# Attention block on one Trainium2 core: residual loads four chains ahead in six buffers, and a later place for the bias on POOL

## The chip, the cores and the metric

The kernel runs on one core of one Trainium2 chip. The metric is the device time of one execution in microseconds; the time before is the median of three runs. The engines are called PE (TensorE, matrix products), DVE (VectorE), ACT (ScalarE), POOL (GpSimd) and SP (SyncE, which here only issues DMAs).

## What is computed

An input x of 4 images with 512 channels and 48 x 48 points goes through a group norm, an attention with 8 heads over the 2304 points of its image, a projection, and is added to the result:

```
hn = _group_norm(x, gn_scale, gn_bias)
qkv = jnp.einsum('oc,bchw->bohw', qkv_w, hn) + qkv_b[None, :, None, None]
...
w = jnp.einsum('bhct,bhcs->bhts', q * scale, k * scale)
w = jax.nn.softmax(w, axis=-1)
a = jnp.einsum('bhts,bhcs->bhct', w, v).astype(jnp.float32)
a = a.reshape(b, c, hh, ww)
out = jnp.einsum('oc,bchw->bohw', proj_w, a) + proj_b[None, :, None, None]
return x + out
```

The change touches the last two lines alone: how x (the residual) and `proj_b` (the bias) get to the projection's result.

## The kernel before

The 8 heads of an image are taken as 4 pairs, so there are 16 pairs in all. A pair's 2304 query points are cut into blocks, four of 512 and one of 256 (`QBLOCKS`). A block is worked off in bursts of three score tiles: six bursts for a block of 512, three for the block of 256. In a burst PE makes scores (L1083), ACT their exponentials (L1090), DVE sums these (`add`, L1139 and L1144), and PE multiplies them with the values two bursts later (L1108). The main loop (L1530) walks through all bursts; `n` is the burst's number, and `now[0]` holds it.

All other work is put beside the bursts from a queue, `beside`, by `fill(n)` (L1477): the products for q, k and v of later pairs, the norm of the next image, and the projection of the image before. The programmer's code fixes the order of all five engines: an engine works off its instructions as the code emitted them, and waits in front of one whose operands are not ready.

When a block is finished, its row sums go a long way round. DVE copies them (`slx`, L1183), SP sends them off by DMA (`sums`, L1186), POOL checks their range in four small steps (`check_sums`, L1205 and L1206, tiles `in` and `tests`), DVE inverts them (L1212), SP sends the inverses to DRAM (`row`, L1214) and back, spread over the partitions (`ib`, L1224), and POOL multiplies (the division, `divide`, L1232). Each step has its burst: check and inversion two bursts after the block, the division two more later.

The projection of a block of 512 points is four chains, one for each 128 output channels; a chain for the block of 256 does two of them. `proj_list` counts them: 18 in an image. A chain is eight matrix products (L970) into one accumulator bank, of which there is only one for all work beside the bursts. Before a block's first chain `begin` (L1023) has ACT and POOL convert the attention's result to the type for four of the products (`att32`, the casts, L960 and L962). After a chain DVE evacuates the bank (L994): it scales the sum and adds it to a residual tile `r` that already holds x plus bias. SP then stores the tile (L997).

The residual tile is made ready thus. `residual` (L904) takes one of `RES` = 4 buffers and has SP load 128 channels of x into it (L915), 256 KB. It then notes in `unbiased` that the bias is due one burst later. `add_bias` (L921) has POOL add it (L926). The main loop calls it near the burst's start (L1545), ahead of the burst's sums, check, division and of `fill`; `proj_run` (L987) calls it at once for a tile that it needs and that has not had its bias yet. The first two loads of an image are issued in `begin` of block 0. Each chain then asks for the load two chains on (`ahead(k + 2)`, L1036), which SP issues in the next burst.

Two more things use these buffers: the projection weights at the start (L568), and one block of the second image (`SPARE`, L509). In the last image three of the five blocks (`in_two`) keep their residual in other buffers, and their loads are issued while the third image is projected, so that POOL then adds two biases a chain. In the tables of the order, `r_0_2` is the residual of block 0, channels from 256 on; the image's number is left out, and the number behind it is the buffer's.

The four projections lie at 637 to 769, 1047 to 1181, 1453 to 1543 and 1545 to 1624 us of the trace. The first three belong to images 0 to 2 and run beside the bursts of the next image; the last is that of image 3.

Of the kernel before, what the change touches and what calls it, by code (L numbers as in the profile page):

```python
# [27 lines left out]
NC = C // P  # L28
# [447 lines left out]
def fast_path(  # L476
# [11 lines left out]
):  # L488
    nc = tc.nc

    RES = NC
    const = ctx.enter_context(tc.tile_pool(name="const", bufs=1))
    xpool = ctx.enter_context(tc.tile_pool(name="xpool", bufs=1))
    qkp = ctx.enter_context(tc.tile_pool(name="qkp", bufs=3))
# [13 lines left out]

    SPARE = {(1, 2): lambda c: ("res", RES), (1, 3): lambda c: (f"a32_{c}", 1)}  # L509

# [56 lines left out]
    def load_wproj(c):  # L567
        wproj[c] = work.tile([P, C], F32, tag="res", bufs=RES, name=f"wproj_{c}")  # L568
        nc.sync.dma_start(wproj[c], proj_wT[bass.ts(c, P), :])
# [314 lines left out]
    now = [0]  # L884
# [14 lines left out]
    def rows_of(dram_tensor, b, j, chunks):  # L899
        o, n = QBLOCKS[j]  # L900
        found = dram_tensor[b, chunks[0] * P : (chunks[-1] + 1) * P, o : o + n]
        return found.rearrange("(m p) n -> p m n", p=P)

    def residual(b, j, chunks):  # L904
        n = QBLOCKS[j][1]
        if in_two(b, j):

            tag = f"x{chunks[0]}_{(j - NQ + 2) % 3}"
            xt = xpool.tile([P, QB], F32, tag=tag, name=f"r_{b}_{j}_{chunks[0]}")
        else:  # L910
            xt = work.tile(
                [P, QB], F32, tag="res", bufs=RES, name=f"r_{b}_{j}_{chunks[0]}"
            )
        xt = xt.rearrange("p (m n) -> p m n", n=n)
        nc.sync.dma_start(xt, rows_of(x, b, j, chunks))  # L915
        res[b, j, chunks[0]] = xt
        unbiased.append((now[0] + 1, (b, j, chunks[0]), chunks))

    unbiased = deque()

    def add_bias():  # L921
        _, key, chunks = unbiased.popleft()
        xt = res[key]
        for i, m in enumerate(chunks):
            bias = bproj[:, m : m + 1].to_broadcast((P, xt.shape[2]))
            nc.gpsimd.tensor_tensor(xt[:, i], xt[:, i], bias, ALU.add)  # L926

    def in_two(b, j):

        return b == B - 1 and j >= NQ - 3  # L930
# [49 lines left out]
    def proj_run(b, j, chunks, pairs=range(NC), bank=None):  # L980

        n = QBLOCKS[j][1]
        if bank is None:
            bank = chain_bank(f"pr_{b}_{j}_{chunks[0]}")
        places = [bank[:, i * n : (i + 1) * n] for i in range(len(chunks))]
        xt = res[b, j, chunks[0]]
        while any(k == (b, j, chunks[0]) for _, k, _ in unbiased):  # L987
            add_bias()
        for m, ps in zip(chunks, places):
            proj_chain(b, j, m, ps, pairs)  # L990

        def evacuate():
            ps = bank[:, : len(chunks) * n].rearrange("p (m n) -> p m n", n=n)
            nc.vector.scalar_tensor_tensor(xt, ps, DOWN, xt, ALU.mult, ALU.add)  # L994

        def store(engine=nc.sync):
            engine.dma_start(rows_of(out, b, j, chunks), xt)  # L997

        return evacuate, store

    def proj_piece(b, j, chunks, pairs=range(NC), ahead=None):
        def run():
            evacuate, store = proj_run(b, j, chunks, pairs)
            evacuate()
            if pairs == LAST:
                finished.add((j, chunks[0]))

            if pairs != FIRST:
                loads.append((now[0] + 1, store))
            if ahead is not None:  # L1010
                loads.append((now[0] + 1, ahead))

        return piece(QB / 290.0 * len(pairs) / NC, run, True, True)

    def proj_pieces(b, j):

        def ahead(k):
            if k < len(proj_list) and not in_two(b, proj_list[k][0]):  # L1020
                residual(b, *proj_list[k])

        def begin():  # L1023
            if in_two(b, j):
                att32(b, j, LAST)
            elif (b, j) == (B - 1, 0):
                att32(b, j, range(len(EARLY), NC))
            else:
                att32(b, j)
            if j == 0:  # L1030
                ahead(0)
                ahead(1)

        pairs = LAST if in_two(b, j) else range(NC)
        chains = [
            proj_piece(b, j, chunks, pairs, lambda k=k: ahead(k + 2))  # L1036
            for k, (jj, chunks) in enumerate(proj_list)
            if jj == j
        ]
        return [piece(0.0, begin)], chains  # L1040
# [293 lines left out]
    for b in range(B):  # L1334
# [20 lines left out]
        if b == B - 1:  # L1355
# [6 lines left out]
            ahead = [  # L1362
                (residual, b, j, chunks)
                for j in (NQ - 2, NQ - 3, NQ - 1)
                for jj, chunks in proj_list
                if jj == j
            ]
# [4 lines left out]
            for j in range(NQ):  # L1372
# [5 lines left out]
            ahead = [  # L1378
                (att32, b, NQ - 3, THIRD),
                (att32, b, NQ - 1, THIRD),  # L1380
                *((att32, b, 0, (c,), True) for c in EARLY),
            ]
# [147 lines left out]
    for n in range(end):  # L1530
        now[0] = n
        idle_once("sync", "scalar", "gpsimd")
        summed = block_at(n - BEHIND - 1)
        if not summed:
            load_due(n)
        wanted(stream[n][0])
        inside = n - BEHIND == soon[1]
        scores(stream[n], (lambda: values(stream[n - BEHIND])) if inside else None)
        if summed:

            rows(*summed, add_up(*summed))
            load_due(n)
        if inside:
            expect_end(kinds.DVE)
        while unbiased and unbiased[0][0] <= n:  # L1545
            add_bias()
        if n > 0:
            add(stream[n - 1])
        filled = summed or n - BEHIND - 1 in soon
        if filled:  # L1550

            fill(n)
        if n >= BEHIND and not inside:
            values(stream[n - BEHIND])
        if block_at(n - BEHIND - 2):
            check_sums(*block_at(n - BEHIND - 2))
            invert(*block_at(n - BEHIND - 2))
        if block_at(n - BEHIND - 3):
            spread(*block_at(n - BEHIND - 3))
        if block_at(n - BEHIND - 4):  # L1560

            divide(*block_at(n - BEHIND - 4))
        if not filled:
            fill(n)
        while joins:
            joins.popleft()()
        if n - BEHIND in soon:
            g, j = stream[n - BEHIND][:2]
            sx = rows(g, j, add_up(g, j))
            if n - BEHIND == soon[1]:  # L1570
                divide_here(g, j, sx, avx[g, j], nc.gpsimd)
        if n - BEHIND - 1 == soon[0]:
            check_sums(g, j)
            invert(g, j)
        if n - BEHIND - 2 == soon[0]:
            spread(g, j)
            divide(g, j)
    g, b, j = NG - 1, B - 1, NQ - 1
    n = QBLOCKS[j][1]
# [18 lines left out]
    ahead, todo = todo[: len(beside)], todo[len(beside) :]  # L1598
# [122 lines left out]
```

## Time and profile before

| | before |
|---|---|
| median of three runs | 1630.75 us |
| lowest and highest run | 1629.93 and 1634.76 us |
| the profiled execution | 1632.66 us |
| its span, first to last instruction | 1630.9 us |
| mean granted clock of PE in it | 0.993 |
| ACT, POOL busy | 1269.4 us, 442.3 us |
| loads of residuals (L915) | 72, median 3.3 us from issue to landing |
| bias additions on POOL (L926) | 80, 93.7 us busy |
| evacuations of projection chains on DVE (L994) | 81 |
| DMA | 82.13 MB, mean 50 GB/s |

A row of the profile's list of waits reads: engine and what it does, for whom it waited, total us, how often, the longest. A row of the timeline has the start in us, the length, the engine, line and operation, out<-in, how many were merged into the row, and in brackets how long the engine had been idle and what ended that. A row of the busy times by stretch has from:to, its length, then for each engine the busy us and the number of instructions, the granted clock of PE, the share of time that the DMA engines were busy, and GB/s. "SPq" is the queue of DMAs that SP issues.

### The profile page before, as it was taken

Reading aid. Unit: us, or ns where it says so; the run is one execution under the profiler, and the core shown is the slowest. Engines: PE = TensorE matmul, PEld = TensorE weight load, DVE = VectorE, ACT = ScalarE, POOL = GpSimd, SP = SyncE. Lnnn points to the kernel's source line nnn. Section 1 sums busy time; section 2 is a strip of 40 time slices with the busy share of each in tenths; the row PEclk is TensorE's granted clock in tenths of the full one; section 3 lists DMA queues with packets and bytes.
Section 4 is the critical chain, followed back from the end, with each engine's and each line's share of the span. In section 5 each row is a group of like instructions: output and inputs, shape, how many; then the busy total and the mean of one; then the engine's idle time right before and its main releaser. Section 6 shows DMA issues by size and latency. Waiting matters only on the chain. (4 is left out here: it accounts for less than half of the span.)

```text
span 1630.9 us, 28897 instructions
## 1 busy us (share of the span) xinstructions
PE 1582.4 (97%) x11526; PEld 681.5 (42%) x11526; DVE 1154.9 (71%) x1302; ACT 1269.4 (78%) x1363; POOL 442.3 (27%) x551
## 2 busy tenths in 40 slices
PE   9988999999999999899999999999999999999896
PEld 3623444443333533445333354444533334434443
DVE  6266768876666668887666666888767676777685
ACT  4166777888888888788888888887878888887784
POOL 1021202311121212642112121354212121128553
PEclk9999999999999999999999999999999999999998
DMA  6001012000000024521000001352100000016323
GB/s 220 1 14 59 15 37 53 12 14 18 14 14 11 15 56 118 147 71 28 11 14 18 14 12 40 114 155 78 31 14 11 14 17 15 14 24 195 114 66 126
DMA packets 94900, 82.13 MB, mean 50 GB/s; under 512 B 50852, under 2 KB 60964, under 8 KB 94756
## 3 DMA queue, kind: packets, MB, share of 16 engines
q1 hardware_dynamic: 92724, 78.35, 17.6%
q8 instruction: 92, 1.51, 0.4%
q10 hardware_dynamic: 1904, 1.84, 0.4%
q14 instruction: 52, 0.43, 0.1%
q0 software_dynamic: 128, 0.01, 0.0%
HBM read 60.70 MB, written 19.17 MB: 49 GB/s over the span
## 5 line engine op out<-in xcount | busy, mean ns | idle before, releaser
L1090 ACT ACTIVATE p<-ps 128x1024 f16<-128x1024 f32 x1296 | 1233.4, 1025 | 329.7 <-PE ps L1083 323.7
L1139 DVE TENSOR_TENSOR acc<-acc,p 128x3072 f16<-128x3072 f16 x270 | 490.5, 1817 | 53.4 <-ACT p L1090 50.8
L812 PE MATMUL pqk<-x,wqkv 128*64 128x512 f32 (+1 forms) x2432 | 514.7, 553 | 4.8 <-DVE k L823 4.7
L1108 PE MATMUL av<-p,v 128*64 128x512 f16 (+1 forms) x2880 | 361.3, 364 | 0.0
L1083 PE MATMUL ps<-q,k 64*128 64x512 f16 (+1 forms) x2880 | 356.5, 358 | 0.4 <-DVE v L872 0.2
L864 PE MATMUL pv<-wqkv,x 128*64 128x256 f32 x2304 | 267.6, 379 | 0.4 <-DVE r L994 0.3
L1205 POOL TENSOR_SCALAR in<-sums 128x8 f32<-128x8 f32 (+1 forms) x158 | 103.5, 655 | 597.8 <-DMA sums<-slx 590.5
L812 PEld LDWEIGHTS pqk<-x,wqkv 128*64 128x64 f32 x2432 | 170.0, 138 | 212.8 <-issue 157.6
L1083 PEld LDWEIGHTS <-k 64*128 64x128 f16 x2880 | 106.6, 94 | 287.8 <-issue 238.4
L1232 POOL TENSOR_TENSOR att<-avx,ib 128x512 f16<-128x512 f32 (+1 forms) x78 | 129.1, 1655 | 355.5 <-DMA ib<-row 334.1
L1108 PEld LDWEIGHTS <-v 128*64 128x64 f16 x2880 | 131.4, 109 | 212.8 <-issue 168.3
L864 PEld LDWEIGHTS pv<-wqkv,x 128*64 128x64 f32 x2304 | 166.2, 137 | 81.9 <-DVE r L994 0.8
L1139 DVE TENSOR_TENSOR acc<-p,p 128x3072 f16<-128x3072 f16 x79 | 142.0, 1797 | 0.0
L1144 DVE TENSOR_TENSOR acc<-acc 128x1024 f16<-128x1024 f16 x156 | 118.6, 760 | 3.3
L926 POOL TENSOR_TENSOR r<-r,bproj 128x512 f32<-128x512 f32 (+1 forms) x80 | 93.7, 1183 | 65.7 <-DMA r<-x_dram 24.5
L823 DVE TENSOR_SCALAR q<-pqk,bqkv 128x512 f16<-128x512 f32 (+1 forms) x77 | 53.4, 694 | 79.2 <-PE pqk L812 78.8
L872 DVE TENSOR_TENSOR v<-pv,bv 128x512 f16<-128x512 f32 x72 | 49.6, 689 | 80.8 <-PE pv L864 80.4
L823 DVE TENSOR_SCALAR k<-pqk,bqkv 128x512 f16<-128x512 f32 (+1 forms) x75 | 52.1, 694 | 74.9 <-PE pqk L812 74.7
L970 PE MATMUL pr<-a,whi 128*128 128x512 f32 (+1 forms) x311 | 96.0, 424 | 4.3 <-POOL a L960 4.2
L970 PE MATMUL pr<-att,wlo 128*128 128x512 f16 (+1 forms) x311 | 76.1, 365 | 19.5 <-DVE r L994 19.1
L1183 DVE COPY slx<-sl 128x512 f32<-128x512 f32 (+1 forms) x79 | 50.5, 640 | 61.8 <-PE sl L1167 61.8
L994 DVE SCALAR_TENSOR_TENSOR r<-pr,r 128x512 f32<-128x512 f32 x75 | 51.4, 686 | 55.7 <-POOL r L926 37.7
(124 smaller groups left out, 544.2 us busy)
## 6 DMA issues: line engine op xcount, KB each, us to landing
r<-x_dram SPq DMA_DIRECT2D x72, 256.0 KB, 3.3
out_dram<-r SPq DMA_DIRECT2D x69, 256.0 KB, 2.3
ib<-row SPq DMA_DIRECT2D x126, 128.0 KB, 3.0
x<-x_dram SPq DMA_DIRECT2D x62, 256.0 KB, 3.9
x<-x_dram SPq DMA_DIRECT2D x16, 128.0 KB, 5.0
sums<-slx SPq DMA_DIRECT2D x128, 2.0 KB, 2.0
ib<-row SPq DMA_DIRECT2D x30, 64.0 KB, 3.1
wqkv<-qkv_wT_dram SPq DMA_DIRECT2D x2, 768.0 KB, 6.9
```

Source lines behind the costliest of these rows:

```text
L812: nc.tensor.matmul(pw[0][lo : lo + D, :n], wqkv[:, c, w0 + lo : w0 + lo + D], hn[b, c, j], start=(c == 0), stop=(c == NC - 1),)
L823: nc.vector.tensor_scalar(qk[g][part][:, o : o + n], pw[0][:, :n], bqkv[:, col : col + 1], SCALE, ALU.add, ALU.mult,)
L864: nc.tensor.matmul(pw[0][lo : lo + D, a, :], hn[b, c, i * P // QB][:, at + lo : at + lo + D], wqkv[:, c, 2 * C + half * C // 2 :][:, : C / ...
L926: nc.gpsimd.tensor_tensor(xt[:, i], xt[:, i], bias, ALU.add)
L970: nc.tensor.matmul(ps[:, :n], w[:, bass.ts(m, P)], a, start=(i == 0), stop=(i == len(steps) - 1),)
L1083: nc.tensor.matmul(ps[:, h, a * n : (a + 1) * n], kt[rows, bass.ts(i, P)], qt[rows, o : o + n], start=True, stop=True,)
L1090: nc.scalar.activation(pt[:, r], ps, AF.Exp)
L1108: nc.tensor.matmul(av[0][lo : lo + D, :n], vv[b, pr // 2][:, i, pr % 2 * P + lo : pr % 2 * P + lo + D], pt[:, r, h, a * n : (a + 1) * n], ...
L1139: nc.vector.tensor_tensor(t, before, pt, ALU.add)
L1144: nc.vector.tensor_tensor(t[:, 0], t[:, 0], t[:, r], ALU.add)
L1205: nc.gpsimd.tensor_scalar(t, sm, limit, None, op)
L1232: nc.gpsimd.tensor_tensor(atts[g][:, o : o + n], avx.pop((g, j))[:, :n], ibs.pop((g, j))[:, :n], ALU.mult,)
```

## The change

There are six residual buffers in place of four. `begin` of block 0 issues the first four loads of an image in place of two, and a chain asks for the load four chains on. The bias is due two bursts after its load in place of one, and the main loop adds due biases after `fill` and the joins, so behind the burst's check, division and casts.

```
-    RES = NC
+    RES = NC + 2
+    LEAD = RES - 2
...
-        unbiased.append((now[0] + 1, (b, j, chunks[0]), chunks))
+        unbiased.append((now[0] + 2, (b, j, chunks[0]), chunks))
...
             if j == 0:
-                ahead(0)
-                ahead(1)
+                for k in range(LEAD):
+                    ahead(k)
...
-            proj_piece(b, j, chunks, pairs, lambda k=k: ahead(k + 2))
+            proj_piece(b, j, chunks, pairs, lambda k=k: ahead(k + LEAD))
...
         if inside:
             expect_end(kinds.DVE)
-        while unbiased and unbiased[0][0] <= n:
-            add_bias()
         if n > 0:
             add(stream[n - 1])
...
         while joins:
             joins.popleft()()
+        while unbiased and unbiased[0][0] <= n:
+            add_bias()
         if n - BEHIND in soon:
```

The lines of the changed kernel are one further on from L916. The order on PE, DVE and ACT is the same in both; it differs on POOL and SP.

On POOL, at the start of the last projection, before:

```order
L960 CAST a_3_0_3_16104<-att_15600 128x512
L926 TENSOR_TENSOR r_0_0_16106<-r_0_0_16106,bproj 128x512
L926 TENSOR_TENSOR r_0_1_16108<-r_0_1_16108,bproj 128x512
L1232 TENSOR_TENSOR att_15600<-avx_1_16004,ib_1_16132 128x512
L926 TENSOR_TENSOR r_0_2_16146<-r_0_2_16146,bproj 128x512
L926 TENSOR_TENSOR r_0_3_16180<-r_0_3_16180,bproj 128x512
```

and in the changed kernel:

```order
L961 CAST a_3_0_3_16104<-att_15604 128x512
L927 TENSOR_TENSOR r_0_0_16106<-r_0_0_16106,bproj 128x512
L1233 TENSOR_TENSOR att_15604<-avx_1_16004,ib_1_16134 128x512
L927 TENSOR_TENSOR r_0_1_16108<-r_0_1_16108,bproj 128x512
L927 TENSOR_TENSOR r_0_2_16110<-r_0_2_16110,bproj 128x512
L927 TENSOR_TENSOR r_0_3_16112<-r_0_3_16112,bproj 128x512
```

The bias of the second chain, `r_0_1`, has moved behind the division of block 1 of the last pair.

A little later on POOL, in block 1 of the last projection, before:

```order
L926 TENSOR_TENSOR r_1_0_16216<-r_1_0_16216,bproj 128x512
L1205 TENSOR_SCALAR in_2_16302<-sums_2_16263 128x8
L1206 TENSOR_TENSOR tests<-tests,in_2_16302 128x8
L1205 TENSOR_SCALAR in_2_16305<-sums_2_16263 128x8
L1206 TENSOR_TENSOR tests<-tests,in_2_16305 128x8
L926 TENSOR_TENSOR r_1_1_16267<-r_1_1_16267,bproj 128x512
L1232 TENSOR_TENSOR att_15600<-avx_2_16238,ib_2_16346 128x512
L926 TENSOR_TENSOR r_1_2_16313<-r_1_2_16313,bproj 128x512
L926 TENSOR_TENSOR r_1_3_16351<-r_1_3_16351,bproj 128x512
```

and in the changed kernel:

```order
L927 TENSOR_TENSOR r_1_0_16149<-r_1_0_16149,bproj 128x512
L927 TENSOR_TENSOR r_1_1_16186<-r_1_1_16186,bproj 128x512
L1206 TENSOR_SCALAR in_2_16307<-sums_2_16268 128x8
L1207 TENSOR_TENSOR tests<-tests,in_2_16307 128x8
L1206 TENSOR_SCALAR in_2_16310<-sums_2_16268 128x8
L1207 TENSOR_TENSOR tests<-tests,in_2_16310 128x8
L927 TENSOR_TENSOR r_1_2_16221<-r_1_2_16221,bproj 128x512
L1233 TENSOR_TENSOR att_15604<-avx_2_16242,ib_2_16349 128x512
L927 TENSOR_TENSOR r_1_3_16272<-r_1_3_16272,bproj 128x512
```

`r_1_1` now stands ahead of the checks and `r_1_2` ahead of the division.

On SP, at the start of the second projection, where `sums_4` carries the row sums of a block to POOL's checks and DVE's inversion, before:

```order
L1224 DMA ib_3_10573<-row_3_10538 64x512 x2
L915 DMA r_0_0_10591<-x_dram 128x512
L915 DMA r_0_1_10593<-x_dram 128x512
L1186 DMA sums_4_10615<-slx_4_10613 128x1x2 x2
L520 DMA x_0_3_10618<-x_dram 128x512
```

and in the changed kernel:

```order
L1225 DMA ib_3_10573<-row_3_10538 64x512 x2
L916 DMA r_0_0_10591<-x_dram 128x512
L916 DMA r_0_1_10593<-x_dram 128x512
L916 DMA r_0_2_10595<-x_dram 128x512
L916 DMA r_0_3_10597<-x_dram 128x512
L1187 DMA sums_4_10619<-slx_4_10617 128x1x2 x2
```

Two more loads stand ahead of `sums_4`. On POOL the first two biases of this projection, which stood ahead of the division and of the checks that wait for `sums_4`, stand behind both in the changed kernel.

## The prediction

> **What bounds the kernel now.** I read the page's busy times first, then the busy times by stage, then the list of waits, then the timeline at the waits that were left.
>
> ```profile
> PE 1582.4 (97%) x11526; PEld 681.5 (42%) x11526; DVE 1154.9 (71%) x1302; ACT 1269.4 (78%) x1363; POOL 442.3 (27%) x551
> ```
>
> TensorE (PE) works for 97% of the span, so only its idle time, 48.5 us of 1630.9, can be won without taking work from it. The next rows say where that idle time lies (from:to in us, length, then the busy time of each engine, TensorE's clock, the DMA share).
>
> ```profile
> 620.00:720.00 100.00, 94.47 (x650) 43.13 (x648) 88.60 (x112) 80.41 (x90) 51.05 (x55) 1.00 0.44 129
> 720.00:1000.00 280.00, 280.00 (x2148) 118.21 (x2146) 192.92 (x200) 232.12 (x245) 54.95 (x76) 1.00 0.08 16
> 1475.00:1512.00 37.00, 31.43 (x190) 14.62 (x188) 26.37 (x24) 28.27 (x33) 34.67 (x30) 1.00 0.64 195
> ```
>
> Between projections (720 to 1000) PE never rests. While a projection runs it does: 5.5 us lost of 100 in the first, 5.6 of 37 in the densest part of the third. The list of waits names the cause (engine and line that wait, for whom, total us, times, longest).
>
> ```profile
> DVE r L994 <- POOL r L926: 37.7, 28, 4.1
> POOL r L926 <- DMA r<-x_dram: 24.5, 13, 7.8
> PE pr L970 <- DVE r L994: 19.1, 17, 2.8
> PE pr L970 <- POOL a L960: 4.2, 5, 1.5
> ```
>
> The chain is load, bias on POOL (L926), evacuation on DVE (L994), next chain on PE (L970), which needs the one accumulator bank back. The 19.1 us is what PE pays. The change is aimed at the first two rows.
>
> **The change part by part.** No instruction is added: 72 loads, 80 bias additions and all work of PE, DVE and ACT stay, in the same order on those three. Only POOL's and SP's orders move. I take the terms in turn.
>
> *The waits that go.* Not all of the 19.1 us comes from a late bias. These rows are the PE waits behind evacuations before which DVE had not been waiting for POOL (start, length, what; in brackets the idle time before it and its cause):
>
> ```profile
> 659.72 1.02 PE L970 MATMUL pr<-att,wlo 128*128 128x512 f16 x4 [0.16 <-DVE r L994]
> ...
> 688.46 1.02 PE L970 MATMUL pr<-att,wlo 128*128 128x512 f16 x4 [2.17 <-DVE r L994]
> ...
> 1070.36 1.02 PE L970 MATMUL pr<-att,wlo 128*128 128x512 f16 x4 [0.41 <-DVE r L994]
> ...
> 1097.11 1.02 PE L970 MATMUL pr<-att,wlo 128*128 128x512 f16 x4 [0.25 <-DVE r L994]
> ...
> 1110.78 1.02 PE L970 MATMUL pr<-att,wlo 128*128 128x512 f16 x4 [1.74 <-DVE r L994]
> ```
>
> They sum to 4.7 and stay: DVE was busy with other work. That leaves 14.4. At two places of the third projection PE waited longer than DVE waited for POOL, so a punctual bias gives back only DVE's part:
>
> ```profile
> 1483.94 0.69 DVE L994 SCALAR_TENSOR_TENSOR r<-pr,r 128x512 f32<-128x512 f32 x1 [0.93 <-POOL r L926]
> ...
> 1484.69 1.02 PE L970 MATMUL pr<-att,wlo 128*128 128x512 f16 x4 [1.71 <-DVE r L994]
> ...
> 1509.52 0.69 DVE L994 SCALAR_TENSOR_TENSOR r<-pr,r 128x512 f32<-128x512 f32 x1 [0.93 <-POOL r L926]
> ...
> 1510.27 1.02 PE L970 MATMUL pr<-att,wlo 128*128 128x512 f16 x4 [1.60 <-DVE r L994]
> ```
>
> That takes off (1.71 - 0.93) + (1.60 - 0.93) = 1.45, to 12.9. One wait is that of the very first chain of the last projection, whose load is issued at the same point as before:
>
> ```profile
> 1577.95 0.69 DVE L994 SCALAR_TENSOR_TENSOR r<-pr,r 128x512 f32<-128x512 f32 x1 [3.08 <-POOL r L926]
> ...
> 1578.69 1.02 PE L970 MATMUL pr<-att,wlo 128*128 128x512 f16 x4 [1.27 <-DVE r L994]
> ```
>
> It stays as well: 11.6 us are won. The same list of waits, for 1380 us to the end alone, has
>
> ```profile
> PE pr L970 <- DVE r L994: 9.8, 7, 2.8
> ```
>
> Without the last projection's two (1.27 and, below, 2.84) the third has 5.7 of it, 4.3 after the 1.45. So the term is at most 14.4, and at least 7.3 if the third projection keeps its waits for the reason of the first rival. I take 11.6, because the loads come two chains earlier, each chain lasting about 3.4 us at this pace (one starts at 1578.69, the next, below, at 1582.10), while POOL waited for a landing 24.5 us in all.
>
> The largest single wait shows what the new place on POOL does. POOL's queue held the division (L1232), which waits for its own DMA, in front of the bias:
>
> ```profile
> 1599.41 1.26 POOL L1232 TENSOR_TENSOR att<-avx,ib 128x512 f16<-128x512 f32 x1 [4.22 <-DMA ib<-row]
> 1600.63 2.03 POOL L926 TENSOR_TENSOR r<-r,bproj 128x512 f32<-128x512 f32 x2
> 1601.70 0.69 DVE L994 SCALAR_TENSOR_TENSOR r<-pr,r 128x512 f32<-128x512 f32 x1 [4.12 <-POOL r L926]
> ...
> 1602.44 1.86 PE L970 MATMUL pr<-att,wlo 128*128 128x512 f16 x4 [2.84 <-DVE r L994]
> ...
> 1603.75 2.01 PE L970 MATMUL pr<-a,whi 128*128 128x512 f32 x4
> ```
>
> In the new order this bias (r_1_2) stands ahead of that division, so the 2.84 us go.
>
> *The clock.* That same chain ran slowly. It took from 1602.44 to 1605.76, 3.32 us; the chain quoted further down, from 1582.10 to 1584.06, took 1.96. The granted clock in that stretch (the number after POOL's) was 0.59:
>
> ```profile
> 1602.00:1606.00 4.00, 3.56 (x14) 2.01 (x15) 2.43 (x3) 0.00 (x0) 0.77 (x2) 0.59 0.18 66
> ```
>
> I take it that the 2.84 us of idling brought the clock down and that without the wait it stays up: 1.4 us won, between 0 and 1.4. [...] I go by the row, since the low clock follows the longest idle time in the projections at once.
>
> *The casts.* PE's 4.2 us for POOL's casts (L960) lie behind biases that waited for a landing, or behind the checks after them. Casts now come ahead of the burst's biases, and POOL no longer stands still for loads. Some casts were also late because the division or the checks were; those stay. I take 1.5 of 4.2, between 0 and 4.2.
>
> *What the new order costs.* A bias that used to run early in its burst now stands behind the burst's division and checks. In the last projection the second chain's bias (r_0_1) moves behind the division:
>
> ```profile
> 1576.88 2.03 POOL L926 TENSOR_TENSOR r<-r,bproj 128x512 f32<-128x512 f32 x2 [1.53 <-DMA r<-x_dram]
> ...
> 1578.87 2.79 POOL L1232 TENSOR_TENSOR att<-avx,ib 128x512 f16<-128x512 f32 x1
> ...
> 1580.74 0.69 DVE L994 SCALAR_TENSOR_TENSOR r<-pr,r 128x512 f32<-128x512 f32 x1 [0.21 <-issue]
> ...
> 1582.10 1.04 PE L970 MATMUL pr<-att,wlo 128*128 128x512 f16 x4
> ...
> 1582.78 1.28 PE L970 MATMUL pr<-a,whi 128*128 128x512 f32 x4
> ```
>
> The division ends at 1581.66; half of the 2.03 us for its bias makes 1582.68, DVE's 0.69 makes 1583.37, and PE wanted the bank at 1582.10: a new wait of 1.3 us. The same rows give the slack that a late evacuation has: it ended at 1581.43, 0.67 us before PE's next chain.
>
> In the second projection two more loads stand on SP ahead of a DMA for which DVE waits, and the first bias stands behind the checks that need this DMA:
>
> ```profile
> 1046.86 1.05 SPq L915 DMA_DIRECT2D r<-x_dram  x2
> ...
> 1048.01 2.36 SPq L1186 DMA_DIRECT2D sums<-slx  x2
> ...
> 1052.71 0.18 DVE L1212 RECIPROCAL inv<-sums 128x4 f32<-128x4 f32 x1 [0.46 <-DMA sums<-slx]
> ...
> 1056.63 0.69 DVE L994 SCALAR_TENSOR_TENSOR r<-pr,r 128x512 f32<-128x512 f32 x1 [0.26 <-issue]
> ...
> 1057.00 0.23 POOL L1205 TENSOR_SCALAR in<-sums 128x4 f32<-128x4 f32 x1
> ...
> 1059.43 0.20 POOL L1206 TENSOR_TENSOR tests<-tests,in 128x4 f32<-128x4 f32 x1
> ```
>
> Two more issues cost 1.05, so the reciprocal goes from 1052.71 to 1053.76: 1.05 - 0.67 = 0.4 on PE. The four checks took 2.63 (1057.00 to 1059.63); 1053.76 + 2.63 + about 1.04 for the bias is 1057.43, 0.8 after the evacuation's 1056.63, or 0.1 past the slack. I take 0.8 for the place, since the bias need not be a fast one:
>
> ```profile
> L926 POOL TENSOR_TENSOR r<-r,bproj x80: 605/1038/2567, 637.2 to 1601.6; 128x512 f32<-128x512 f32 x64, 128x256 f32<-128x256 f32 x16
> ```
>
> Its slowest is 1.5 us over the median. The third projection's first two biases move behind such checks as well; 0.4, by the same arithmetic. Together 2.5. At best 0; with a slowest bias at each of the three places 1.3 + 0.5 + 3 x 1.5 = 6.3.
>
> The two extra buffers cost nothing: load k+4 takes the buffer of chain k-2, as load k+2 did with four, so each load waits for the same store as before. The loads' issue time on SP is otherwise the same, in another order; SP stands mostly waiting for DVE.
>
> **The rivals.**
>
> *POOL itself is full.* From 1475 to 1512 POOL is busy for 34.67 of 37 us (the row above): there it adds two biases a chain, one for this projection and one for the last batch's. If its throughput, not the landing of loads, makes the bias late, earlier loads win nothing there: 4.3 of the 11.6 stay, and so does the 1.5 of the casts. That gives 12.0 - 5.8 = 6.2 us, 1624.6. For it: the spread of one bias from 0.6 to 2.6 us, so POOL is often held up. Against it: POOL's order now does this projection's biases first. [...] Chance 0.18.
>
> *The wait changes its name.* PE stops waiting for DVE and waits for casts or for DVE's other work instead, so that the stage keeps its pace: 4.9 us or less won, 1626 to 1635. For it: the 4.7 us of waits behind a busy DVE. Against: DVE loses 37.7 us of waiting. Chance 0.10.
>
> *Slower: the bias sits behind a division that waits.*
>
> ```profile
> POOL att L1232 <- DMA ib<-row: 334.1, 62, 9.4
> ```
>
> One such wait is 5.4 us on average. If in each of the four projections a chain's evacuation meets it, 5.4 less the slack of 0.67 is 4.7, four times 18.9 us; with the gain that is 6.9 slower, 1637.7. It decides where a division stands ahead of a bias whose evacuation is due before the division's DMA lands. The new order has this at one place only, the one costed at 1.3. Chance 0.04.
>
> **How the numbers follow.** 11.6 + 1.4 + 1.5 - 2.5 = 12.0 us. The profiled execution took 1632.66 (span 1630.9), 1.9 above the median of 1630.75; 1632.66 - 12.0 = 1620.7, and against the median 1618.8. Forecast 0.68. About 0.3%, 4.9 us, is what a measurement here can tell from no change. Faster: forecast and first rival, 0.86; the same 0.10; slower 0.04. All bounds at once would give 14.4 + 1.4 + 4.2 = 20 us (1610.8) and 7.3 - 6.3 = 1.0 us (1629.8); they will not all meet, so the range is 1613 to 1627, which holds the forecast and the first rival.
>
> **What would show it.** Right: PE's wait for L994 falls from 19.1 to about 9 (4.7, 1.45, 1.27 and the new ones), POOL's wait for the loads goes from 24.5 to under 5, the 2.84 us wait near the end is gone and the clock stays up there, and a new wait of about 1.3 stands at the last projection's third chain. Wrong: PE's wait for L994 over 14, or its wait for the casts well above 4.2, or POOL's busy share at the third projection unchanged with DVE still waiting for it.

## The result, and the profile after

The changed kernel takes 1620.89 us (median of six runs, 1619.39 to 1623.05), the kernel before 1630.34 beside it (six runs, 1628.48 to 1634.76): 9.5 us less, a ratio of 0.994 with a 95% interval of 0.9927 to 0.9954. The forecast was 1618.8 in a range of 1613 to 1627. The profiled execution has a span of 1620.3 us, 10.6 less than before.

The busy times, the group of the bias additions and the list of waits of the changed kernel. Its lines are one further on: the bias is L927, the evacuation L995, the projection's products L971, the casts L961.

```profile
PE 1581.4 (98%) x11526; PEld 681.4 (42%) x11526; DVE 1151.4 (71%) x1302; ACT 1269.6 (78%) x1363; POOL 453.4 (28%) x551
...
L927 POOL TENSOR_TENSOR r<-r,bproj 128x512 f32<-128x512 f32 (+1 forms) x80 | 108.2, 1376 | 1.7 <-DMA r<-x_dram 1.7
```

```profile
DVE r L995 <- POOL r L927: 27.5, 18, 3.2
...
PE pr L971 <- DVE r L995: 11.5, 13, 2.2
...
PE pr L971 <- POOL a L961: 2.0, 3, 0.9
...
POOL r L927 <- DMA r<-x_dram: 1.7, 1, 1.7
...
PE pr L971 <- DVE q L824: 0.7, 1, 0.7
```

POOL hardly waits for a load any more (24.5 us before, 1.7 now). PE's waits for evacuations fell from 19.1 to 11.5, those for casts from 4.2 to 2.0; 0.7 for another tile of DVE's is new. That is 7.6 + 2.2 - 0.7 = 9.1 us, and PE is busy for 1.0 less: 10.1 of the 10.6. Two things did not go as one might think. DVE still waits 27.5 us for biases, of 37.7, and the 80 biases themselves became slower, 108.2 us of POOL where the page of before has 93.7 us.

The busy times by stage, in the stretches shown of before and two more:

```profile
620.00:720.00 100.00, 97.00 (x662) 44.11 (x660) 89.77 (x115) 81.36 (x91) 53.15 (x56) 0.98 0.44 129
...
1475.00:1512.00 37.00, 33.86 (x225) 16.26 (x224) 28.59 (x27) 30.78 (x38) 36.55 (x31) 1.00 0.61 192
...
1590.00:1594.00 4.00, 4.00 (x24) 2.02 (x23) 2.62 (x3) 3.50 (x5) 1.84 (x1) 1.00 0.47 177
...
688.00:692.00 4.00, 4.00 (x17) 1.31 (x15) 2.73 (x4) 3.04 (x5) 2.83 (x4) 0.57 0.63 194
```

PE gained 2.4 us in the third projection's densest part, though POOL is now busy for 36.55 of 37 us there. The chain that ran at half rate from 1602.44 before (granted clock 0.50 from 1602 to 1605) now starts at 1592.52, without a wait ahead of it and at full clock (the third row, 1.00); the stretch of half rate at 688 (the last row, 0.50 from 689 to 691) is one that the kernel before did not have.

### The profile page after: what moved, and what is told of

Its sections match the earlier page's. It is cut to its first block, busy times and chain, and to the rows that moved or that the text cites. A ratio compares the mean times of both kernels' runs of the same rounds, so it can differ in the third digit from the quotient of the medians.

```text
span 1620.3 us, 28874 instructions
## 1 busy us (share of the span) xinstructions
PE 1581.4 (98%) x11526; PEld 681.4 (42%) x11526; DVE 1151.4 (71%) x1302; ACT 1269.6 (78%) x1363; POOL 453.4 (28%) x551
## 5 line engine op out<-in xcount | busy, mean ns | idle before, releaser
L1206 POOL TENSOR_SCALAR in<-sums 128x8 f32<-128x8 f32 (+1 forms) x158 | 100.2, 634 | 616.2 <-DMA sums<-slx 609.2
L1145 DVE TENSOR_TENSOR acc<-acc 128x1024 f16<-128x1024 f16 x156 | 114.6, 735 | 3.3
L824 DVE TENSOR_SCALAR q<-pqk,bqkv 128x512 f16<-128x512 f32 (+1 forms) x77 | 53.4, 694 | 81.2 <-PE pqk L813 80.8
L927 POOL TENSOR_TENSOR r<-r,bproj 128x512 f32<-128x512 f32 (+1 forms) x80 | 108.2, 1376 | 1.7 <-DMA r<-x_dram 1.7
L824 DVE TENSOR_SCALAR k<-pqk,bqkv 128x512 f16<-128x512 f32 (+1 forms) x75 | 52.1, 694 | 76.0 <-PE pqk L813 75.8
L971 PE MATMUL pr<-a,whi 128*128 128x512 f32 (+1 forms) x311 | 95.3, 422 | 2.1 <-POOL a L961 2.0
L971 PE MATMUL pr<-att,wlo 128*128 128x512 f16 (+1 forms) x311 | 74.8, 360 | 12.5 <-DVE r L995 11.5
L995 DVE SCALAR_TENSOR_TENSOR r<-pr,r 128x512 f32<-128x512 f32 x75 | 51.4, 685 | 42.7 <-POOL r L927 27.5
```

What stands on the lines that cost most here:

```text
L824: nc.vector.tensor_scalar(qk[g][part][:, o : o + n], pw[0][:, :n], bqkv[:, col : col + 1], SCALE, ALU.add, ALU.mult,)
L971: nc.tensor.matmul(ps[:, :n], w[:, bass.ts(m, P)], a, start=(i == 0), stop=(i == len(steps) - 1),)
L1145: nc.vector.tensor_tensor(t[:, 0], t[:, 0], t[:, r], ALU.add)
L1206: nc.gpsimd.tensor_scalar(t, sm, limit, None, op)
```

## The experiments

All times are medians of the same kind, the ratio is to the kernel before on the same chip. Beside these kernels the one before measured 1629.2 to 1630.3 us, so times of rows that did not run together compare to about 1 us, and the ratios compare better.

| kernel | us | ratio, 95% interval |
|---|---|---|
| changed kernel | 1620.9 | 0.994 (0.9927 to 0.9954) |
| loads alone | 1618.6 | 0.994 (0.9928 to 0.9953) |
| place alone, due two bursts on | 1637.9 | 1.0047 (1.0035 to 1.006) |
| place alone, due one burst on | 1634.0 | 1.003 (1.0018 to 1.0042) |
| old place, due two bursts on, loads early | 1619.2 | 0.9936 (0.9923 to 0.9948) |
| due biases ahead of checks and divisions | 1618.5 | 0.9932 (0.9918 to 0.9946) |
| last image's biases deferred | 1617.6 | 0.9927 (0.9914 to 0.9939) |
| loads alone, last image's biases deferred | 1616.8 | 0.9924 (0.9911 to 0.9938) |
| loads alone, three chains ahead | 1621.1 | 0.9952 (0.9938 to 0.9966) |
| no bias | 1603.6 | 0.9845 (0.9831 to 0.9858) |
| bias on ACT | 1611.2 | 0.9895 (0.988 to 0.991) |
| bias on ACT, its casts on POOL | 1609.9 | 0.9882 (0.9867 to 0.9897) |

### Loads alone

```
+    RES = NC + 2
+    LEAD = RES - 2
...
         unbiased.append((now[0] + 1, (b, j, chunks[0]), chunks))
...
+                for k in range(LEAD):
+                    ahead(k)
```

The main loop keeps the bias at its old place.

> The change's loads alone: six buffers and loads four chains ahead, but the bias due one burst after its load and at its old place, near the burst's start. Theory A (the loads were too late, their earlier issue is what pays): most of the gain stays, 1620 to 1624 us, PE's waits for the evacuation 10 to 13 us; POOL may still stand 3 to 10 us in front of a load, but a chain or more before the evacuation needs the tile. Theory B (the place pays, because POOL no longer does a bias ahead of casts, checks and divisions): little of the gain, 1627 to 1631 us, PE's waits for the casts at 4 us or more.

Measured: 1618.63 us. All of the gain is there without the new place; theory A stands, and the time is even below its range. Its waits:

```profile
POOL r L927 <- DMA r<-x_dram: 22.5, 11, 5.2
...
PE pr L971 <- POOL a L961: 6.2, 5, 1.8
PE pr L971 <- DVE r L995: 6.1, 9, 1.4
...
DVE r L995 <- POOL r L927: 5.3, 4, 3.1
```

POOL still stands 22.5 us in front of loads, nearly as long as before, but it does so well ahead of need: DVE waits for biases for 5.3 us, before 37.7. In return POOL's casts are late, 6.2 us of PE's time. Theory A had expected 10 to 13 us of waits for evacuations, where 6.1 are left, and 3 to 10 us of POOL's in front of loads. What mattered here was not that POOL waited but for whom it was late.

### Place alone

The second run takes the first one's other half: `RES = NC` and `LEAD = RES - 2`, so four buffers and two chains, with the bias due two bursts on, behind the burst's other work.

> The change's place alone: four buffers and loads two chains ahead as before, but the bias due two bursts after its load, behind the burst's other work on POOL. Theory A (late loads): the loads land as late as before, so the evacuations go on waiting; 1627 to 1632 us, PE's waits for the evacuation 15 us or more. Theory B (the place): 1621 to 1625 us, and PE's waits for the casts fall to about 2 us.

Measured: 1637.89 us, 7.8 slower than the kernel before. Theory B falls, and theory A had the price too small. One place of it, a part of its timeline in the third projection:

```profile
1484.19 1.27 POOL L1233 TENSOR_TENSOR att<-avx,ib 128x512 f16<-128x512 f32 x1 [4.24 <-DMA ib<-row]
1485.41 5.55 POOL L927 TENSOR_TENSOR r<-r,bproj 128x512 f32<-128x512 f32 x4
1487.48 0.69 DVE L995 SCALAR_TENSOR_TENSOR r<-pr,r 128x512 f32<-128x512 f32 x1 [5.82 <-POOL r L927]
1488.22 1.87 PE L971 MATMUL pr<-att,wlo 128*128 128x512 f16 x4 [4.07 <-DVE r L995]
```

POOL stands 4.24 us in front of a division whose DMA is not there; the bias behind it comes late by that much, and PE loses 4.07 us. This is the mechanism of the prediction's slower rival. With loads four chains ahead the same queue does much less harm (the changed kernel's longest wait of PE behind such a division is 1.07 us, shown further down): there a bias is due two chains further ahead of its evacuation.

The bias's due time was changed together with its place; the next run takes it back:

```
-        unbiased.append((now[0] + 2, (b, j, chunks[0]), chunks))
+        unbiased.append((now[0] + 1, (b, j, chunks[0]), chunks))
```

> The change's place alone, as in the run before that was slower than the kernel before by 7.8 us (1637.9), but with the bias due one burst after its load again. If the loss comes from the second burst of delay (the bias is then issued only when its chain asks for it): 1629 to 1632 us, about the kernel before. If it comes from the place behind the burst's checks, division and casts: 1634 to 1640 us, and PE's waits for evacuations above 23 us.

Measured: 1634.01 us, PE's waits for evacuations 25.7 us. The place loses time by itself, 4.9 us against the kernel before beside it. With the second burst of delay the loss was 7.8; the intervals of the two ratios overlap, so what that burst adds is not shown.

### Old place with the late due time

The changed kernel with the two lines of `add_bias` in the main loop put back ahead of `add`.

> Six buffers, loads four chains ahead, bias due two bursts after its load, but at the old place near the burst's start, ahead of the burst's checks and division. In the changed kernel the bias additions took 108.2 us on POOL in all, before 93.7; 17 of the 80 took about 2.5 us, before 4 or so. Theory A (late loads were the cause, and the late place costs: it puts the bias beside VectorE's big additions and behind divisions): 1617 to 1620 us, bias additions under 100 us, no PE wait of about 1 us at the last projection's second and third chains. Theory B (the late place is part of the gain): 1623 to 1627 us, with more PE waits for casts or evacuations than in the changed kernel.

Measured: 1619.17 us, so the late place is no part of the gain. The intervals of this run, the loads alone and the changed kernel overlap: with loads this early, place and due time move the time by less than these runs can tell. Of the changed kernel's two waits of about 1 us at the start of the last projection, which theory A expected to go, one is left (1.02 us at 1568.81). One number of theory A was wrong. The biases did not get shorter at the old place:

```profile
L927 POOL TENSOR_TENSOR r<-r,bproj 128x512 f32<-128x512 f32 (+1 forms) x80 | 110.8, 1405 | 6.9 <-DMA r<-x_dram 3.9 <-DVE st L635 1.2 <-issue 0.9
```

### Why biases are late in the third projection

In the changed kernel eight evacuations there follow their bias at once, with loads that had landed 7 to 14 us before the bias began. Theory C says that POOL is full. Theory D came from its rows in the timeline:

```profile
1465.21 1.06 POOL L1206 TENSOR_SCALAR in<-sums 128x8 f32<-128x8 f32 x1 [10.23 <-DMA sums<-slx]
...
1467.11 8.16 POOL L927 TENSOR_TENSOR r<-r,bproj 128x512 f32<-128x512 f32 x5
```

POOL stood idle for 10.23 us in front of a check, with four biases queued behind it, and then did five in a row, for 8.16 us.

For theory C, the last image's biases get a queue of their own, `spare`, which only `proj_run` empties:

```
-        unbiased.append((now[0] + 2, (b, j, chunks[0]), chunks))
+        (spare if in_two(b, j) else unbiased).append((now[0] + 2, (b, j, chunks[0]), chunks))
...
+        while any(k == (b, j, chunks[0]) for _, k, _ in spare):
+            add_bias(spare)
```

> The changed kernel, with one edit: the ten bias additions of the last image that POOL did beside the third projection are taken out of it and done by POOL just ahead of the first chains that use these tiles, after the third projection. In the changed kernel eight evacuations of the third projection follow their bias at once, although the loads had landed 5 to 14 us before, and POOL was busy for 36.55 of 37 us there. Theory C (POOL itself is full in the third projection, the rest of the waits there is its doing): PE's waits in the third projection, 2.0 us for evacuations and 2.0 us for casts, fall under 1 us together, and the time to 1616 to 1618.5 us. Otherwise (the waits there come from elsewhere, or the ten additions cost as much where they now stand): 1620 to 1622 us.

Measured: 1617.64 us. PE's waits from 1453 to 1536 us:

```profile
PE pr L971 <- DVE r L997: 0.9, 2, 0.5
PE pr L971 <- POOL a L961: 0.6, 1, 0.6
```

and from 1536 to 1568, where these biases now stand just ahead of their chains:

```profile
PE pr L971 <- DVE r L997: 4.5, 5, 1.5
```

The third projection went from 4.0 to 1.5 us of waits, more than theory C's "under 1", and 4.5 us came in later. Over the whole program the two waits sum to 13.9 us, in the changed kernel to 13.5, so by them it should not have been faster. That it measures 3 us less lies at the edge of what the intervals tell apart. In the two profiled executions PE idles equally long, 38.9 us; the whole 5.3 us between their spans is PE's busy time. 2.0 of that are the clock's in the projections: this execution has no stretch of half rate behind the projections' waits (a granted clock of 1.00 in every us from 600 to 1600), the changed kernel's has one, and the projections' products took 168.1 us where they took 170.1 there (rows in the last section). It is therefore no proof for theory C.

For theory D, due biases stand ahead of the check or division in the bursts that have one:

```
+        if block_at(n - BEHIND - 2) or block_at(n - BEHIND - 4):
+            while unbiased and unbiased[0][0] <= n:
+                add_bias()
         if block_at(n - BEHIND - 2):
             check_sums(*block_at(n - BEHIND - 2))
```

> The changed kernel with one edit: in a burst in which POOL has a check or a division, the biases that are due stand ahead of it, as the old place had them; in all other bursts they keep the new place. Theory D (the new place costs because POOL stands in front of checks that wait for sums, 10.23 us at 1465 of the changed kernel, with four landed loads queued behind them, and the third projection starts with that backlog): PE's waits for evacuations and casts in the third projection fall from 4.0 us to under 2.5, the waits of 1.44 and 1.07 us at the start of the last projection to about one of them, and the time to 1616 to 1619 us. Theory C (POOL is full there whatever the order): 1620 to 1622 us, the third projection's waits as in the changed kernel.

Measured: 1618.46 us. The idle time in front of the check fell and the four biases are done ahead of it:

```profile
1455.13 6.46 POOL L927 TENSOR_TENSOR r<-r,bproj 128x512 f32<-128x512 f32 x4
1465.40 1.06 POOL L1206 TENSOR_SCALAR in<-sums 128x8 f32<-128x8 f32 x1 [3.81 <-DMA sums<-slx]
```

PE's waits from 1453 to 1543 us in this kernel are

```profile
PE pr L971 <- POOL a L961: 1.7, 4, 0.6
...
PE pr L971 <- DVE r L995: 0.9, 2, 0.7
```

2.6 us, where the changed kernel has 2.0 + 2.0 = 4.0; theory D expected under 2.5. Of the two waits at the start of the last projection one is left, 1.25 us, as it expected. The backlog is shown in the rows; its price in these waits is some 1.4 us. The time lies in theory D's range, but its interval overlaps that of the changed kernel. Part of the waits is left with either order, so a share for theory C isn't ruled out.

### Both together

The loads alone, the queue `spare`, and in the main loop

```
+        if spare and not unbiased and spare[0][0] <= n:
+            add_bias(spare)
```

> The loads alone (six buffers, four chains ahead, bias one burst after its load at the old place), and with it the ten bias additions of the last image moved out of the third projection: POOL does one of them at the end of a burst in which no other bias is noted, so from about 1525 us on. The kernel with the loads alone had 5.2 us of PE waits for POOL's casts in the third projection (1.71, 1.83 and 1.65). If the casts were late because POOL still had biases of the last image ahead of them, two of the three go, and the time falls from 1618.6 to 1614 to 1616.5 us. If the casts are late for another reason (they wait for PE to free their tile, or for a division), it stays at 1618 to 1620 us.

Measured: 1616.80 us, just above the expected range. PE's waits for casts fell from 6.2 to 2.8 us, as expected, but those for evacuations rose from 6.1 to 7.7. It is the best version that leaves the bias on POOL, by a margin over the loads alone that the intervals do not confirm.

### Three chains ahead

The loads alone with `RES = NC + 1`.

> The loads alone, with five buffers and three chains ahead instead of six and four; bias one burst after its load at the old place. With four chains ahead the biases were ready 3 to 14 us before their evacuations in the second and third projections; one chain is about 3.4 us. Theory A (it is enough that the load lands before its bias is due): 1618 to 1621 us, as with four. If the fourth chain is needed: 1623 to 1627 us, between two chains (1630) and four (1618.6).

Measured: 1621.06 us, the upper end of theory A's range. PE's waits for evacuations are 6.0 us, as with four chains (6.1). The step from two chains to three is what counts; a worth of the fourth isn't shown.

### Without the bias

`add_bias` only takes the entry from the queue, and no bias is added.

> The changed kernel without the 80 bias additions: proj_b is left out of the result. It shows what all of them still cost. The changed kernel's PE waits for evacuations sum to 11.5 us; about 4.7 of them lie behind a busy VectorE, which needs no bias to explain it. If the other 6.8 us and the 2.0 us for casts are the biases' doing, and nothing else takes their place: 1611 to 1614 us, PE's waits for evacuations 4 to 6 us. If a wait for the loads themselves or for VectorE takes their place: 1616 to 1620 us.

Measured: 1603.61 us, far below what either theory expected. The 11.5 us of waits for evacuations are gone, the 4.7 behind a busy DVE with them. From its list of waits:

```profile
PE pr L972 <- DVE r L996: 0.2, 1, 0.2
```

The waits that went (11.3, 2.0 for casts, the 0.7 for DVE's other tile) and 4.8 us of PE's busy time (1576.6) make 18.8 of the 19.0 by which the span is shorter; 2.2 of the 4.8 lie in the projections' products (170.1 us, here 167.9), with a granted clock of 1.00 in every us from 600 to 1595. So DVE was not busy on its own account. The place of the longest of these waits, in the changed kernel's timeline:

```profile
681.28 1.75 DVE L1140 TENSOR_TENSOR acc<-acc,p 128x3072 f16<-128x3072 f16 x1
681.43 2.50 POOL L927 TENSOR_TENSOR r<-r,bproj 128x512 f32<-128x512 f32 x1
...
682.95 1.02 DVE L668 COPY both<-rstd 128x32 f32<-128x32 f32 x1
...
684.58 1.03 POOL L927 TENSOR_TENSOR r<-r,bproj 128x512 f32<-128x512 f32 x1
684.67 0.96 DVE L679 TENSOR_TENSOR mga<-cols,ga 128x4 f32<-128x4 f32 x1
...
686.33 0.68 DVE L995 SCALAR_TENSOR_TENSOR r<-pr,r 128x512 f32<-128x512 f32 x1
```

and the same two small instructions without a bias:

```profile
680.77 0.17 DVE L668 COPY both<-rstd 128x32 f32<-128x32 f32 x1
...
681.46 0.16 DVE L679 TENSOR_TENSOR mga<-cols,ga 128x4 f32<-128x4 f32 x1
```

The copy of 0.17 us takes 1.02 and ends 0.04 after POOL's bias does; the product of 0.16 takes 0.96 and ends 0.02 after the next bias. The other way round, the bias that starts inside DVE's 1.75 us addition takes 2.50 us and ends 0.90 after the addition; the next one, which starts ahead of DVE's product, takes 1.03. In these rows the instruction that starts second is held up until the other has ended. Not every pair shows this: the evacuation of 0.69 us that DVE starts at 1587.74, inside a bias of 1.04 us, is no longer than the others (0.63 to 0.69 us for all 75). The same two long instructions stand in the kernel before, ahead of the same 2.17 us wait:

```profile
684.34 1.02 DVE L667 COPY both<-rstd 128x32 f32<-128x32 f32 x1
...
686.07 0.96 DVE L678 TENSOR_TENSOR mga<-cols,ga 128x4 f32<-128x4 f32 x1
```

So the trace that the prediction read could have shown it.

### The bias on ACT

The regular tiles' bias moves to ACT, one a burst; the last image's ten stay on POOL in the queue `spare`.

```
+            if in_two(*key[:2]):
+                nc.gpsimd.tensor_tensor(xt[:, i], xt[:, i], bias, ALU.add)
+            else:
+                bias = bproj[:, m : m + 1]
+                nc.scalar.activation(xt[:, i], xt[:, i], AF.Identity, bias=bias)
```

> The changed kernel with the 62 regular bias steps moved from POOL to ACT (an activation with the bias, one step at a burst's end); the ten of the last image stay on POOL. Without any bias the kernel took 1603.6 us, 17 less than the changed kernel, because POOL's additions and VectorE's instructions hold each other up (a 0.17 us copy on VectorE took 1.02 beside a bias, a bias 2.5 instead of 1.04 beside VectorE's additions). Theory E (it is this contention, and not POOL's queue alone): 1606 to 1611 us, VectorE's waits for biases under 6 us. Rival (ACT has no room: from 1475 to 1512 it is busy for 30.78 of 37 us, and eleven steps of about 0.6 us, the price of ACT's casts, are 6.6 us more than the 6.2 that are free): PE waits for the exponentials, 1615 to 1625 us.

Measured: 1611.17 us, 18 less than the kernel before (ratio 0.9895). ACT's group and PE's new wait:

```profile
L931 ACT ACTIVATE r<-r,bproj 128x512 f32<-128x512 f32 (+1 forms) x68 | 50.9, 772 | 1.1 <-DMA r<-x_dram 1.1
```

```profile
PE ps L1090 <- ACT p L1097: 4.1, 10, 0.5
...
PE pr L975 <- DVE r L1001: 1.7, 3, 0.8
```

That is just above theory E's range, and DVE's waits for biases, now from ACT, are 7.0 us where it expected under 6; the gain is there all the same. The run takes 68 of the 80 biases out of POOL's queue and from beside DVE's instructions at once, so it does not tell what each of the two costs. The rival has its share: from 1475 to 1512 us ACT is busy without a pause.

```profile
1475.00:1512.00 37.00, 35.03 (x238) 17.60 (x238) 28.15 (x28) 37.00 (x49) 19.61 (x22) 1.00 0.56 172
```

The last run gives POOL ACT's casts too, all four of a block, or two of them where POOL has a division:

```
-        return range(NC - 1 if divided[0] == now[0] else NC // 2, NC)
+        return range(NC // 2 if divided[0] == now[0] else 0, NC)
```

> As the run before, with the casts that ACT does in the projections given to POOL as well (two of four of a block; one of two where POOL has a division), so that ACT gets back about half of what the biases take. Theory E: as the run before or up to 3 us better if ACT was short of room there, 1604 to 1610 us. Rival (casts on POOL contend with VectorE as the biases did and are late, as PE's 2 to 6 us of waits for POOL's casts in the earlier runs suggest): 1612 to 1618 us, with PE's waits for POOL's casts above 5 us.

Measured: 1609.89 us, the fastest kernel with the whole result: 19.3 us under the kernel before, where the changed one won 9.5. The same stretch, and PE's waits in it and elsewhere:

```profile
1475.00:1512.00 37.00, 36.32 (x248) 17.61 (x248) 29.64 (x31) 34.34 (x40) 29.15 (x34) 1.00 0.59 182
```

```profile
PE pr L975 <- POOL a L965: 1.6, 4, 0.5
...
PE pr L975 <- DVE r L1001: 1.3, 3, 0.7
...
PE ps L1090 <- ACT p L1097: 0.3, 1, 0.3
```

The waits for the exponentials are nearly gone. Those for POOL's casts, of which the run before had none, come to 1.6 us, far from the rival's 5. Against the run before, the 1.3 us are less than the intervals can tell.

## Why the prediction was right, point by point

The forecast was 12.0 us less; the two profiled executions differ by 10.6, the medians by 9.5. The main term, the late loads, was right in its cause. The terms for the clock and for the new place came near their numbers by luck, as said there.

- **Late biases, less the new waits: forecast 11.6 - 2.5 = 9.1 us, measured 7.6 - 0.7 = 6.9.** The cause was the right one: loads issued earlier give the whole gain by themselves, and the place gives none. The size was 2.2 too large. With the new 0.7 counted, the waits left are above the forecast by 0.6 us in the first projection, 0.6 in the second, 0.2 in the third and 0.8 in the last. Nearly all waits that are left go when the bias goes, so they are the biases' doing, by POOL's queue or by the hold-ups between POOL and DVE.
- **"They sum to 4.7 and stay: DVE was busy with other work."** Behind the same five chains 4.5 us are left (0, 2.17, 0, 0.91 and 1.38), so the sum was right to leave them out, but the reason was wrong: the run without biases has none of them. DVE was held up by POOL, as the rows show for the largest; for the others the rows of that run are the evidence. The list of the prediction also misses two of its kind, 0.28 at 682.81 and 0.34 at 695.26, which it counted as won; 0.28 and 0.19 of them are left.
- **The 2.84 us near the end** are gone. The prediction put that down to the bias standing ahead of the division. The kernel with the loads alone has no such wait either, with the bias at its old place: its last wait of PE for an evacuation is 1.3 us at 1568.66. So the early load is enough.
- **The clock: forecast 1.4, about 2 measured.** Before there were two stretches of half rate beside the projections, now there is one, and the projections' products fell from 172.1 to 170.1 us (last section). PE's other work took 1.0 more, so its busy time fell by 1.0 only. The forecast meant the stretch at 1602, which is gone; one at 1537 is gone too, and one at 688 is new. That the balance came near the forecast is luck.
- **The casts: forecast 1.5, measured 2.2**, inside its bounds. Earlier loads do not give this: alone they have 6.2 us of these waits, more than the 4.2 before. It is the later bias that lets the casts go first (2.8 with the late due time at the old place, 2.0 at the new one), and it pays for that in the evacuations.
- **The costs of the new place.** The wait of 1.3 us behind the division in the last projection came, with 1.07:

```profile
1571.53 1.28 POOL L1233 TENSOR_TENSOR att<-avx,ib 128x512 f16<-128x512 f32 x1 [2.27 <-DMA ib<-row]
1572.76 4.55 POOL L927 TENSOR_TENSOR r<-r,bproj 128x512 f32<-128x512 f32 x3
1573.84 0.69 DVE L995 SCALAR_TENSOR_TENSOR r<-pr,r 128x512 f32<-128x512 f32 x1 [2.19 <-POOL r L927]
1574.58 1.02 PE L971 MATMUL pr<-att,wlo 128*128 128x512 f16 x4 [1.07 <-DVE r L995]
```

  The prediction said that the new order has one such place only. There is a second in its own table of the order: `r_1_3` behind the division, which cost PE 0.42 us at 1596.43. In the second projection the cost came by another way than the evacuation: the reciprocal went from 1052.71 to 1053.59, as forecast (1053.76), the tile of q that DVE evacuates behind it came late with it, and PE waited 0.66 us for that tile at 1054.79, which is the new wait for L824. The 0.4 of the third projection did not show: no such wait of PE stands at its start. The loads alone, which have none of these costs, measured 2.3 us less than the changed kernel, with intervals that overlap. That this is near the forecast of 2.5 is luck: they have 5.4 us less of waits for evacuations and 4.2 more for casts.
- **POOL is full (the first rival).** Its sign was there: from 1475 to 1512 us POOL is busier than before, and DVE's wait for it in the whole third projection fell only from 18.3 to 17.2 us. But PE's waits fell from 5.7 to 2.0 for evacuations there and from 2.4 to 2.0 for casts, so the gain came. The sign was badly chosen: DVE's wait cost PE nothing where the evacuation still ended before PE's next chain, so 17.2 us of DVE's waits stand beside 2.0 of PE's. A share of the rival may be true; its experiments leave it open.
  The spread of one bias from 0.6 us, which the prediction held for this rival, is one of sizes at its lower end: the 0.6 are additions of 128x256.
- **The slower rival** had a real mechanism: with loads two chains ahead it costs 4.07 us of PE's time at the place shown, in a kernel of 1637.9 us.

## What to carry to other kernels

The late loads were cured here by issuing them earlier: 1618.6 us by that alone, against 1630.1. Moving their consumer back in a queue that holds waiting instructions only traded one wait for another, and cost 7.8 us while the loads were still just in time. Before work is called another engine's own, its instructions' durations are worth a look: a small one that took six times its usual time (1.02 us for 0.17) was held up here. If POOL and DVE share a stage, moving elementwise work from POOL to ACT can be worth more than the orders of the same work that were tried: 18 us here, and 19 with ACT's casts on POOL, where the best of those won 12.

## What the runs showed of the hardware

**The clock does not follow the length of the last wait alone.** At the same instruction PE had waited 2.17 us in both kernels, at 688.46 before and at 687.06 after. The clock from 688 to 692 us, and at a low place of before that the prediction does not show, was before

```profile
688.00:692.00 4.00, 3.54 (x21) 1.62 (x21) 3.97 (x5) 2.25 (x4) 1.58 (x2) 1.00 0.42 131
1537.00:1541.00 4.00, 4.00 (x22) 1.86 (x19) 2.36 (x2) 2.85 (x3) 3.10 (x4) 0.57 0.34 95
```

so 1.00 behind that wait, where the changed kernel has 0.57, and 0.57 behind a shorter one of 1.54 us at 1535.20. With the last image's biases deferred, too, PE's longest wait for an evacuation, 2.2 us, left no stretch of half rate: the granted clock is 1.00 in every us from 600 to 1600. So it fell after idle times of 1.54, 2.17 and 2.84 us, and stayed up after 2.17 and 2.2. What else decides wasn't tried. What one such stretch costs can be read from the product groups of three executions, with two, one and none of them, before, after and with the last image's biases deferred:

```profile
L970 PE MATMUL pr<-a,whi 128*128 128x512 f32 (+1 forms) x311 | 96.0, 424 | 4.3 <-POOL a L960 4.2
L970 PE MATMUL pr<-att,wlo 128*128 128x512 f16 (+1 forms) x311 | 76.1, 365 | 19.5 <-DVE r L994 19.1
```

```profile
L971 PE MATMUL pr<-a,whi 128*128 128x512 f32 (+1 forms) x311 | 95.3, 422 | 2.1 <-POOL a L961 2.0
...
L971 PE MATMUL pr<-att,wlo 128*128 128x512 f16 (+1 forms) x311 | 74.8, 360 | 12.5 <-DVE r L995 11.5
```

```profile
L971 PE MATMUL pr<-a,whi 128*128 128x512 f32 (+1 forms) x311 | 93.3, 418 | 0.6 <-POOL a L961 0.6
L971 PE MATMUL pr<-att,wlo 128*128 128x512 f16 (+1 forms) x311 | 74.8, 360 | 13.5 <-DVE r L997 13.3
```

The sums are 172.1, 170.1 and 168.1: 2.0 us of the projections' products for each.

**POOL and DVE held each other up.** The copy and the product above took 0.85 and 0.80 us longer beside one bias each, and a bias 1.5 us longer beside one addition. All biases together cost some 16 us (25.5 us are won without them, 9.5 with them, against the kernel before) in a kernel in which POOL is busy for 28% of the span. How much of that is these hold-ups and how much POOL's queue isn't shown.
